# Two transformer blocks on one core: the first attention moves issued ahead of the biases, batch 1's first norm moved behind the first maxima and onto GpSimd, one cross load two rounds later

## The chip, the cores and the metric

The kernel runs on one core of one Trainium2 chip. A core has five engines, each with its own instruction queue: TensorE (PE, matrix products; PEld is its weight load), VectorE (DVE), ScalarE (ACT), GpSimd (POOL) and SyncE (SP, which here only issues DMAs). ACT and POOL can issue DMAs as well. Instructions of one queue run in the order written; between queues, semaphores order them. The metric is the device time of one execution in microseconds (us), lower is better.

## The reference

Two layers, each with self attention, cross attention and a gated feed-forward, every one behind a layer norm and with a residual. 4 batches of 512 tokens, 320 wide; 20 heads of 16; a context of 1601 rows of 192 for the cross attention; all float32.

```python
h1 = _ln(x, n1_g, n1_b)
x = _attn(h1, h1, q1, k1, v1, o1_w, o1_b, heads) + x
h2 = _ln(x, n2_g, n2_b)
x = _attn(h2, context, q2, k2, v2, o2_w, o2_b, heads) + x
h3 = _ln(x, n3_g, n3_b)
proj = h3 @ ff_w1 + ff_b1
a, g = jnp.split(proj, 2, axis=-1)
ff = a * jax.nn.gelu(g, approximate=False) @ ff_w2 + ff_b2
return ff + x
```

## The kernel before, in words

A program in Python writes the instruction order of every engine out by hand. An attention is cut into **units**: one batch and one group of four heads (five groups per batch, so 20 units of self and 20 of cross attention per layer). A unit goes through these steps:

- `add_proj`: queries and keys from the normed tokens (`qkps`, L908). The result is split into a high and a low half in the tile `halves` (L919 and L920 for the very first unit, L924 with POOL's L827 and L828 for the others) and moved by DMA into the layout of the products, `kT` and `q` (L876, "the moves").
- `add_values`: the values (`vps`, L1035, copied into `vals` at L1017), two parts of 4 pieces each for a batch: 128 wide, then 192 wide.
- `max_pairs` / `round_of`: a first pass of score products (`sps`, L1076) that serves only for the maxima of the rows, taken by DVE (L1087). A round of self attention is 8 products and 4 maxima; a unit has 4 rounds.
- `max_end`: the negated maxima are split, turned (L1163) and moved by four small DMAs into `nrows` (L1171).
- `main`: the scores again (`st`, L1324) with the maxima added by a third product that reads `nrows`, the exponential on ACT (L1334), then probabilities times values (`av`, L1350), summed by ACT (L1364, L1369) and POOL (L1370). The pass of maxima of the next unit is woven in between.
- `add_finish`: once the five units of a batch are done, the sums are inverted, and three loads (`aT` L1224 with `rT` L1225, issued by SP) bring the output back; POOL divides (L1232), PE projects (`ops`, L1250). There are only two buffers for `rT`, so the third load waits until POOL has divided the first; what stands behind it in SP's queue waits with it.

`add_norm` makes the layer norm. For the first self attention: statistics (DVE, L561 and L562), an inverse root by a guess and three refinements (`guess_root`, `better_root`, L521 to L537), `plain` (L625, twelve pieces that subtract and scale), and `turn` (L639, twelve transposes by PE into `hps`, brought to `hT` by ACT and DVE at L647 and L645). `biased` (L618) adds the output bias to the residual on POOL. The flag `start["on"]` holds during the beginning and puts root and `plain` on DVE; afterwards they are POOL's.

After the beginning, work is taken from chains by due times counted in **rounds** (two rounds to a step of `main`); a task may also ask that so many rounds have passed since another, as `since(i, n)` does in `add_finish`. The beginning itself, at the end of the function, is a list of calls in order: load batch 0 and the weights, two bias rows (`brow`) and batch 1; norm, project and move unit 0; then unit 1, the norm of batch 1, unit 2, the four rounds of unit 0's maxima with products in between, two rounds of unit 1, and from there the main loop.

Of the kernel before, what the change touches and what calls it, by code (L numbers as in the profile page):

```python
# [23 lines left out]
P = 128  # L24
NQ = N // P
# [53 lines left out]
def kernel(ctx: ExitStack, tc: tile.TileContext, x, context, ws, out):  # L79
# [18 lines left out]
    nc = tc.nc  # L98
# [109 lines left out]
    def now(fs):  # L208
        for f in fs:
            f()  # L210
# [153 lines left out]
    units = []  # L364
# [48 lines left out]
    def bank(name):  # L413
        i = min(range(NB), key=lambda i: bank_free[i])
        assert bank_free[i] < HELD, name
        t = psum.tile([P, 512], F32, tag=f"bank{i}", name=name)
        bank_of[id(t)] = [i, t, bank_free[i], 0.0]
        bank_free[i] = HELD
        return t

    def written(us, *tiles):
        expect["pe"] = max([expect["pe"]] + [bank_of[id(t)][2] + 0.05 for t in tiles]) + us
        for t in tiles:
            bank_of[id(t)][3] = expect["pe"] + 0.17
# [17 lines left out]
    def add(chain, cost, f, due, ready=yes, soon=yes):  # L442
        chains[chain].append((cost if isinstance(cost, tuple) else (cost,), due, ready, soon, f))
# [71 lines left out]
            assert chains[name], name  # L515
            run(name)

    def guess_root(var):

        a, h, y, z = (two.tile([P, NQ], F32, tag=f"root{i}", name=f"root{i}") for i in range(4))  # L520
        nc.vector.tensor_scalar(a, var, EPS, None, ALU.add)  # L521
        nc.vector.tensor_scalar(
            z.bitcast(I32), a.bitcast(I32), 1, None, ALU.logical_shift_right
        )
        nc.vector.tensor_scalar(y.bitcast(I32), z.bitcast(I32), -1, 0x5F3759DF, ALU.mult, ALU.add)
        eng = nc.vector if start["on"] else nc.gpsimd
        eng.tensor_scalar(h, a, -0.5, None, ALU.mult)
        return h, y, z

    def better_root(h, y, z):  # L530


        eng = nc.vector if start["on"] else nc.gpsimd
        eng.tensor_tensor(z, y, y, ALU.mult)
        eng.tensor_tensor(z, z, h, ALU.mult)
        eng.tensor_scalar(z, z, 1.5, None, ALU.add)
        eng.tensor_tensor(y, y, z, ALU.mult)  # L537

    hn_used = []
    EARLIER = 14  # L540


# [8 lines left out]
    def add_norm(l, b, i, put, done, due):  # L551
# [12 lines left out]

        def root(step):
            if step == 0:
                s["root"] = guess_root(s["mv"][:, :, 1])
                s["rstd"] = s["root"][1]
            for _ in range(step + 1):
                better_root(*s["root"])  # L570
            s["round"] = clock["round"]

        def normalise(t):
# [43 lines left out]
        def biased(t):  # L617
            nc.gpsimd.tensor_tensor(xb[:, t, :], xb[:, t, :], brow[(3 * l + i) % 2], ALU.add)  # L618

        def plain(t):  # L620
            if t == 0:
                s["hn"] = one.tile([P, DB, NQ, SLOT], F32, tag="hturned", name="hturned").rearrange("p k t w -> p (k t w)")
            for k, at, n in HK:
                w = n // SLOT
                (nc.vector if start["on"] else nc.gpsimd).tensor_scalar(  # L625
                    s["hn"][:, t * D + at : t * D + at + n].rearrange("p (d k) -> p k d", k=w),
                    xb[:, t, at : at + n].rearrange("p (k d) -> p k d", k=w),
                    s["mv"][:, t, 0:1], s["rstd"][:, t : t + 1], ALU.subtract, ALU.mult,
                )
            if start["on"]:  # L630
                busy("dve", 0.45)
            s["round"] = clock["round"]

        def turn(k, at, n):
            if k == 0:
                place()
            ps = bank("hps")
            for t in range(NQ):
                nc.tensor.transpose(ps[:n, t * P : (t + 1) * P], s["hn"][:, t * D + at : t * D + at + n], ident)  # L639
            written(0.5, ps)  # L640
            busy("act", 0.7, ps)
            to = s["hT"][:n, k].rearrange("p (i t w) -> p t i w", t=NQ, w=SLOT)
            src = ps[:n].rearrange("p (t i w) -> p t i w", t=NQ, w=SLOT)
            if start["on"] and k == 1:
                nc.vector.tensor_scalar(to, src, lng[i][:n, k : k + 1], lnb[i][:n, k : k + 1], ALU.mult, ALU.add)  # L645
            else:
                nc.scalar.activation(to, src, AF.Identity, bias=lnb[i][:n, k : k + 1], scale=lng[i][:n, k : k + 1])  # L647
            if k == 2:
                for t in range(NQ):
                    biased(t)  # L650
                hn_used.remove(b)
                put(s["hT"])

# [498 lines left out]
    def max_end(u):  # L1152

        top, high, low = (u.nm[:, :, i, :] for i in range(3))
        nc.vector.tensor_reduce(
            high.bitcast(F32R), top.rearrange("p j (t o) -> p j t o", o=1), AX.X, ALU.max, negate=True
        )
        nc.vector.tensor_reduce(
            low, u.nm[:, :, 0:2, :].rearrange("p j e t -> p j t e"), AX.X, ALU.add, negate=True
        )  # L1160
        turned = two.tile([P, SLOT], F32, tag="turned", name="turned")

        nc.vector.transpose(turned.rearrange("p (j c) -> p j c", j=HG), u.nm[:, :, 1:3, :].rearrange("p j e t -> p j (e t)"))  # L1163
        busy("dve", 0.6)
        slots = u.rows.bitcast(F32).rearrange("(g s) n -> s g n", s=DH)[0].rearrange("g (t r) -> g t r", t=NQ)

        def rows():
            for i in range(P // SLOT):
                part = slice(i * SLOT, (i + 1) * SLOT)
                queue = (nc.sync, nc.scalar, nc.gpsimd, nc.sync)[i] if start["on"] else nc.sync  # L1170
                queue.dma_start(out=slots[:, :, part], in_=turned[part, :])  # L1171

        if u.cross and u.before.cross:
            u.rows_of = rows
            errands.appendleft((clock["round"] + 1, yes, rows))
        else:
            rows()

    def add_finish(u):
# [3 lines left out]
        def since(i, n):  # L1183
            return lambda: len(when) > i and clock["round"] >= when[i] + n
# [29 lines left out]
        def read():  # L1214

            held["read"] += 1
            held["open"] += 1
            aT = one.tile([P, 3, N], F32, tag="aT", name="aT")
            way, part = o_way[u.b % 2], {}

            def load(k, at, n):
                heads = slice(at // DH, (at + n) // DH)
                part[k] = two.tile([P, N], F32, tag="rT", name="rT")
                dma(out=aT[:n, k, :], in_=way[:DH, heads])  # L1224
                dma(  # L1225
                    out=part[k][:n],
                    in_=r_way[u.b % 2][heads].rearrange("(o j) n -> o j n", o=1).to_broadcast([DH, n // DH, N]),
                )
                when.append(clock["round"])

            def divide(k, n):
                nc.gpsimd.tensor_tensor(aT[:n, k, :], aT[:n, k, :], part[k][:n], ALU.mult)  # L1232

            for k, at, n in DK[:2]:
                load(k, at, n)
            first, second, third = DK
            add("divide", 0.0, lambda: divide(0, first[2]), r - 20, yes, since(4, 3))
            add("divide", 0.0, lambda: divide(1, second[2]), r - 20)
            add("divide", 0.0, lambda: load(*third), r - 20, yes, since(4, 5 if u.l else 7))
            add("divide", 0.0, lambda: divide(2, third[2]), r - 20, yes, since(5, 3))  # L1240
            add("divide", 0.0, lambda: end(aT), r - 20)

# [440 lines left out]
    take_rooms(0)  # L1683
    now(load_x(0))
    now(load_self(0))
    load_bias(0, 0)
    load_bias(0, 1)
    now(load_x(1))

    add_norms(0)  # L1690
    add_proj(units[0])
    warm(5)
    until(lambda: not chains["proj"], "proj")
    at_once(units[0])
    add_proj(units[1])
    add_values(units[0])
    run("proj")
    run("proj")
    for _ in range(2 * NQ + 2):
        run("norm")  # L1700
    at_once(units[1])
    add_proj(units[2])
    first = units[0]
    first.pairs = max_pairs(first)
    for chain in ("proj", "proj", "values", None):
        round_of(first.pairs[0].popleft()[1] + first.pairs[1].popleft()[1])
        if chain:
            run(chain)

    at_once(units[2])  # L1710
    run("values")
    max_reduce(first)
    max_end(first)
    loads.extend(load_x(2))
    for fs in (load_out(0, "o1_w"), load_x(3), load_cross(0)):
        loads.extend(fs)
    second = units[1]
    second.pairs = max_pairs(second)
    for _ in range(2):
        round_of(second.pairs[0].popleft()[1] + second.pairs[1].popleft()[1])  # L1720
        run("values")
        run("values")
    start["on"] = False
    clock["credit"] = 0.0

# [47 lines left out]
```

## Time and profile before

| what | value |
|---|---|
| median of 3 runs | 2929.41 us (2924.77 to 2933.03) |
| the profiled execution | 2929.68 us, of which the span from first to last instruction is 2927.9 us |
| PE busy | 2863.1 us, 98% of the span |
| first 100 us of the span | PE busy 86.94 us, granted clock 0.88 |

Times in the profile count from the start of the span. In rows of the timeline stand: start, length, engine, line, operation, output<-inputs, shapes, count, and in brackets the idle time of that engine before and what ended it. Rows with a count join neighbours of one kind. In rows of the windows stand: the stretch, its length, busy time and instructions of PE, PEld, DVE, ACT and POOL, the clock granted to PE (1.00 is full), the share of the 16 DMA engines that was busy, and GB/s. The engine called SPq or ACTq is that engine's queue, whose rows are DMA issues.

### The profile page before, as it was taken

The page shows a single profiled execution, that of the slowest core. Times are in us where ns is not written, and L with a number is a line of the kernel's source. Part 1 is how long each engine was busy: PE and PEld are TensorE (multiplying, and loading weights), DVE is VectorE, ACT ScalarE, POOL GpSimd, SP SyncE. Part 2 cuts the span into 40 slices and gives each one's busy share as a digit, 9 for nine tenths or more (in the row PEclk, how much of TensorE's full clock was granted, in tenths as well). Part 3 has the DMA queues.
Part 4 walks back from the last instruction along what each step waited for, and adds up shares of the span by engine and source line. Part 5 has one row for each costly group of instructions (what it writes and reads, how often), then busy time and mean ns, then how long its engine had stood idle before and what let it go on. Part 6 is the DMA issues. An engine that isn't in the chain of part 4 may idle for free.

```text
span 2927.9 us, 83288 instructions
## 1 busy us (share of the span) xinstructions
PE 2863.1 (98%) x35018; PEld 1545.3 (53%) x35018; DVE 1980.7 (68%) x3752; ACT 1950.1 (67%) x4033; POOL 1299.5 (44%) x1409
## 2 busy tenths in 40 slices
PE   8999999999999999999999999999999999999999
PEld 4445555555555555355554555555555555544554
DVE  7776878788788878323257678788778888762221
ACT  3777678887888888500138776788888888893000
POOL 3556345555555645211125653455455564451110
PEclk8999999999999999999999999999999999999999
DMA  3443224232232222200113432221122122122000
GB/s 106 111 123 98 67 71 105 59 82 63 51 92 62 54 54 62 84 18 11 36 44 88 109 98 66 68 65 49 54 65 50 47 72 63 42 59 72 20 23 14
DMA packets 163494, 188.59 MB, mean 64 GB/s; under 512 B 61988, under 2 KB 109104, under 8 KB 163120
## 3 DMA queue, kind: packets, MB, share of 16 engines
q1 hardware_dynamic: 162616, 181.69, 24.3%
q8 instruction: 275, 4.51, 0.6%
q10 hardware_dynamic: 472, 1.58, 0.2%
q14 instruction: 99, 0.81, 0.1%
q0 software_dynamic: 32, 0.00, 0.0%
HBM read 55.76 MB, written 29.36 MB: 29 GB/s over the span
## 4 chain that ended last, share of the span: by engine, by line
PE 85%; DVE 6%; POOL 4%; issue 2%; DMA 2%; ACT 1%; SPq 1%; POOLq 0%; ACTq 0%; DVEq 0%
PE av L1350 21%; PE st L1324 19%; PE fps L1435 10%; PE sps L1076 8%; PE yps L1542 6%; PE vps L1035 5%; PE ops L1250 3%; PE kps L972 3%; PE qkps L908 3%; PE fps L1495 3%; DVE nmax L1087 2%; DVE pm L1087 2%; PE qps L947 2%; POOL o L1370 1%; PE sps L1101 1%
## 5 line engine op out<-in xcount | busy, mean ns | idle before, releaser
L1334 ACT ACTIVATE pr<-st 128x512 f32<-128x512 f32 (+1 forms) x2720 | 1404.5, 604 | 327.1 <-PE st L1324 297.0
L1087 DVE TENSOR_REDUCE pm<-sps 128x1 f32<-128x512 f32 (+1 forms) x1920 | 1149.0, 660 | 251.0 <-PE sps L1076 243.8
L1370 POOL TENSOR_TENSOR o<-o,vo 128x512 f32<-128x512 f32 x576 | 739.8, 1284 | 936.9 <-ACT vo L1369 922.1
L1076 PE MATMUL sps<-kT,q 32*128 32x450 f32 (+1 forms) x4800 | 870.7, 422 | 10.7 <-DMA q<-halves 4.3
L1324 PE MATMUL st<-q,kT 32*128 32x512 f32 (+1 forms) x5120 | 791.1, 420 | 2.0 <-ACT o L1364 1.6
L1350 PE MATMUL av<-pr,vals 128*32 128x512 f32 (+1 forms) x5440 | 734.8, 606 | 30.7 <-DVE pm L1087 7.2
L1324 PEld LDWEIGHTS st<-q,kT 32*128 32x128 f32 (+1 forms) x5120 | 448.6, 180 | 293.9 <-ACT pr L1334 115.4
L1324 PE MATMUL st<-nrows,ones 32*128 32x512 f32 (+1 forms) x2720 | 560.8, 398 | 7.1 <-DMA nrows<-turned 7.0
L1087 DVE TENSOR_REDUCE nmax<-sps 128x1 f32<-128x512 f32 x640 | 397.2, 682 | 120.6 <-PE sps L1076 115.2
L1076 PEld LDWEIGHTS sps<-kT,q 32*128 32x128 f32 x4800 | 434.6, 184 | 69.5 <-ACT pr L1334 12.8
L1369 ACT COPY vo<-av 128x512 f32<-128x512 f32 x576 | 352.9, 613 | 15.2 <-PE av L1350 8.5
L1506 ACT ACTIVATE gl<-fps,b 128x512 f32<-128x512 f32 x80 | 54.7, 687 | 409.0 <-PE fps L1495 301.1
L1435 PE MATMUL fps<-hT,w 128*128 128x512 f32 x640 | 283.5, 597 | 0.0
L1324 PEld LDWEIGHTS st<-nrows,ones 32*128 32x128 f32 (+1 forms) x2720 | 263.3, 180 | 18.7 <-issue 6.2
L1350 PEld LDWEIGHTS av<-pr,vals 128*32 128x32 f32 (+1 forms) x5440 | 110.9, 108 | 304.3 <-DVE pm L1087 186.7
L1507 DVE SCALAR_TENSOR_TENSOR hid<-fps,b,gl 128x512 f32<-128x512 f32 x80 | 59.7, 748 | 247.5 <-ACT gl L1506 245.4
L1435 PEld LDWEIGHTS fps<-hT,w 128*128 128x128 f32 x640 | 119.1, 190 | 155.0 <-issue 152.3
L1542 PE MATMUL yps<-w,hid 128*128 128x320 f32 x640 | 175.7, 434 | 0.0
L1542 PEld LDWEIGHTS yps<-w,hid 128*128 128x128 f32 x640 | 120.5, 190 | 56.3 <-ACT gl L1506 5.3
L1250 PEld LDWEIGHTS ops<-wo,aT 112*32 112x32 f32 (+1 forms) x3072 | 97.9, 110 | 61.9 <-issue 30.0
L1250 PE MATMUL ops<-wo,aT 112*32 112x160 f32 (+1 forms) x3072 | 124.9, 300 | 4.1 <-POOL aT L1232 3.8
L1111 DVE TENSOR_REDUCE pm<-sps 128x4 f32<-128x508 f32 x160 | 98.9, 681 | 36.1 <-PE sps L1101 33.0
(89 smaller groups left out, 2459.5 us busy)
## 6 DMA issues: line engine op xcount, KB each, us to landing
kT<-stages SPq DMA_DIRECT2D x80, 400.5 KB
oway<-o SPq DMA_DIRECT2D x80, 256.0 KB
q<-halves SPq DMA_DIRECT2D x80, 256.0 KB
q<-halves SPq DMA_DIRECT2D x27, 512.0 KB
kT<-halves SPq DMA_DIRECT2D x40, 256.0 KB
aT<-oway SPq DMA_DIRECT2D x32, 224.0 KB
rT<-rway SPq DMA_DIRECT2D x32, 224.0 KB
hT<-hturned SPq DMA_DIRECT2D x96, 64.0 KB
```

Source lines behind the costliest of these rows:

```text
L1035: nc.tensor.matmul(ps[f : f + m, :w], lhsT=u.kvT[:n, k, at + f : at + f + m], rhs=wv[:n, k, h0 * DH : h1 * DH], start=(k == 0), stop=(k == ...
L1076: nc.tensor.matmul(own[0][:, :w], lhsT=u.queries(slice(j * SLOT, (j + 1) * SLOT), e, t), rhs=u.kT[j * SLOT : (j + 1) * SLOT, u.k0 + at : u ...
L1087: nc.vector.tensor_reduce(to, own[0][:, :w], AX.X, ALU.max)
L1111: nc.vector.tensor_reduce(u.pm[:, :, j, ns - 1], ps[:, : NQ * w].rearrange("p (t w) -> p t w", w=w)[:, :, :n], AX.X, ALU.max,)
L1250: nc.tensor.matmul(ps[f : f + m, : D // 2], lhsT=aT[:n, k, f * NQ + t * SLOT : f * NQ + t * SLOT + m], rhs=wo[:n, k, cols], start=(k == 0) ...
L1324: nc.tensor.matmul(own[0][:r, :], lhsT=ones[rows, :r] if e == 2 else u.keys(rows, c), rhs=u.rows[rows, :] if e == 2 else u.queries(rows, e ...
L1334: nc.scalar.activation(p[:r], own[0][:r], AF.Exp)
L1350: nc.tensor.matmul(ps[j * SLOT : (j + 1) * SLOT, :], lhsT=columns_of[:r, head : head + SLOT], rhs=pr.pop((c, j))[:r, :], start=True, stop= ...
L1369: nc.scalar.copy(vo, ps)
L1370: nc.gpsimd.tensor_tensor(u.o, u.o, vo, ALU.add)
L1435: nc.tensor.matmul(ps, lhsT=w1[:, k, i * FF + c * P : i * FF + (c + 1) * P], rhs=natural(u.hT[:, k]), start=start, stop=stop,)
L1542: nc.tensor.matmul(ps[:, :D], lhsT=hid[c][:, t * P : (t + 1) * P], rhs=w2[:, c, :], start=(c == 0), stop=(c == NHC - 1),)
```

## The change

- In the beginning, the two `brow` loads and batch 1's four tiles of tokens are issued behind unit 0's moves instead of before them.
- More products by PE whose result nobody reads (`wps`): 7 in place of 5 at the start, and one between the transposes of batch 0's first chunk (three in all).
- All four first pieces of values stand directly behind the projections of units 0 and 1, ahead of the first round of maxima; the two 192-wide pieces that were in the beginning are left to the main loop.
- Batch 1's norm is cut out of its place ahead of the maxima. Its statistics stand on DVE behind unit 0's `max_end`; its root and its twelve pieces of `plain` are on POOL.
- Batch 0's additions of the bias row are held back behind unit 1's moves.
- One round of unit 1's maxima, rather than two, stands ahead of the main loop.
- The first `nrows` are moved by SP and ACT, two each, in place of SP, ACT, POOL, SP.
- In `add_finish`, the third load of layer 1's cross attention is issued 7 rounds behind the first two in place of 5 (layer 0 had 7 already).

```diff
@@ guess_root(var, b), better_root(h, y, z, b)
-        eng = nc.vector if start["on"] else nc.gpsimd
+        eng = nc.vector if start["on"] and not b else nc.gpsimd
...
@@ plain(t)
-                (nc.vector if start["on"] else nc.gpsimd).tensor_scalar(
+                (nc.vector if start["on"] and not b else nc.gpsimd).tensor_scalar(
...
@@ turn(k, at, n)
             ps = bank("hps")
+            idle = bank("wps") if start["on"] and k == 0 else None
             for t in range(NQ):
                 nc.tensor.transpose(ps[:n, t * P : (t + 1) * P], s["hn"][:, t * D + at : t * D + at + n], ident)
+                if idle is not None and t + 1 < NQ:
+                    nc.tensor.matmul(idle[:, :P], lhsT=ident, rhs=fill[:, :P], start=True, stop=True)
+            if idle is not None:
+                busy("act", 0.0, idle)
...
                 for t in range(NQ):
-                    biased(t)
+                    if start["on"] and not b:
+                        held_back.append(lambda t=t: biased(t))
+                    else:
+                        biased(t)
...
@@ max_end(u)
-                queue = (nc.sync, nc.scalar, nc.gpsimd, nc.sync)[i] if start["on"] else nc.sync
+                queue = nc.scalar if start["on"] and i % 2 else nc.sync
...
@@ add_finish(u)
-            add("divide", 0.0, lambda: load(*third), r - 20, yes, since(4, 5 if u.l else 7))
+            add("divide", 0.0, lambda: load(*third), r - 20, yes, since(4, 5 if u.l and not u.cross else 7))
...
@@ the beginning
     now(load_x(0))
     now(load_self(0))
-    load_bias(0, 0)
-    load_bias(0, 1)
-    now(load_x(1))
 
     add_norms(0)
     add_proj(units[0])
-    warm(5)
+    warm(7)
     until(lambda: not chains["proj"], "proj")
     at_once(units[0])
     add_proj(units[1])
     add_values(units[0])
+    load_bias(0, 0)
+    load_bias(0, 1)
+    now(load_x(1))
     run("proj")
     run("proj")
-    for _ in range(2 * NQ + 2):
-        run("norm")
+    for _ in range(4):
+        run("values")
     at_once(units[1])
+    for f in held_back:
+        f()
     add_proj(units[2])
     first = units[0]
     first.pairs = max_pairs(first)
-    for chain in ("proj", "proj", "values", None):
+    for chain in ("proj", "proj", None, None):
         round_of(first.pairs[0].popleft()[1] + first.pairs[1].popleft()[1])
         if chain:
             run(chain)
 
-    at_once(units[2])
-    run("values")
     max_reduce(first)
     max_end(first)
+    at_once(units[2])
+    for _ in range(6):
+        run("norm")
...
-    for _ in range(2):
+    for _ in range(1):
         round_of(second.pairs[0].popleft()[1] + second.pairs[1].popleft()[1])
-        run("values")
-        run("values")
+    for _ in range(10-6):
+        run("norm")
```

The change also moves every later line number by up to 12. Three places show what it does to the queues. First, DVE around unit 0's maxima (`nmax_95`), before; `x_108` is batch 1:

```order
L625 TENSOR_SCALAR hturned<-x_108,mv,root_318 128x4x32
L625 TENSOR_SCALAR hturned<-x_108,mv,root_318 128x3x32 x2
L1087 TENSOR_REDUCE nmax_95<-sps 128x1 x16
L1155 TENSOR_REDUCE nmax_95<-nmax_95 128x4x4
L1158 TENSOR_REDUCE nmax_95<-nmax_95 128x4x4
L1163 STREAM_TRANSPOSE turned<-nmax_95 128x32
```

Here batch 1's norm (its last two rows are shown) stands ahead of the sixteen maxima. The same place on DVE now:

```order
L929 SCALAR_TENSOR_TENSOR halves<-qkps,scales,halves 128x256 x2
L1096 TENSOR_REDUCE nmax_95<-sps 128x1 x16
L1164 TENSOR_REDUCE nmax_95<-nmax_95 128x4x4
L1167 TENSOR_REDUCE nmax_95<-nmax_95 128x4x4
L1172 STREAM_TRANSPOSE turned<-nmax_95 128x32
L562 BN_STATS st_473<-x_108 128x6
L563 BN_AGGR mv<-st_473 128x2
```

The maxima follow the first unit's split directly, and batch 1's statistics come behind them. Its root, the first of three refinements, now on POOL behind unit 2's split:

```order
L837 TENSOR_TENSOR halves<-halves 128x512
L527 TENSOR_SCALAR root_486<-root_485 128x4
L534 TENSOR_TENSOR root_488<-root_487 128x4
L535 TENSOR_TENSOR root_488<-root_488,root_486 128x4
L536 TENSOR_SCALAR root_488<-root_488 128x4
L537 TENSOR_TENSOR root_487<-root_487,root_488 128x4
```

Two more refinements, the twelve pieces L626 and the four additions L619 follow on POOL; none of these but the additions was POOL's before.

Second, PE behind batch 0's transposes (`q_102` and `q_103` are the queries of units 0 and 1), now:

```order
L641 MATMUL hps<-ident,hturned 96x128 x8
L917 MATMUL qkps<-hT,wqk 32x256 x48
L1044 MATMUL vps<-wv_112,hT 32x128 x48
L1085 MATMUL sps<-kT_101,q_102 128x512 x8
L917 MATMUL qkps<-hT,wqk 32x256 x12
```

The four pieces of values (L1044), which were spread between the rounds of maxima, fill the place ahead of the first round. Further on, PE's rows around batch 1's transposes, now:

```order
L1333 MATMUL st<-nrows_97,ones 128x512 x2
L1085 MATMUL sps<-kT_101,q_103 128x512 x2
L641 MATMUL hps<-ident,hturned 128x128 x4
L641 MATMUL hps<-ident,hturned 96x128 x8
L1333 MATMUL st<-q_102,kT_101 128x512 x2
```

The transposes `hps` of batch 1 stand where they stood before: behind the first scores of unit 0 and ahead of all the rest of the main loop.

Third, SP at the end of a batch in layer 1's cross attention, before:

```order
L1225 DMA rT<-rway_132 112x1x512
L1224 DMA aT<-oway_130 96x1x512
L1225 DMA rT<-rway_132 96x1x512
L1171 DMA nrows_97<-turned 8x4x32 x4
L1191 DMA oway_131<-o 4x32x512
```

The next unit's `nrows` stand behind the third load (96 partitions). The same place now:

```order
L1234 DMA rT<-rway_132 112x1x512
L1180 DMA nrows_97<-turned 8x4x32 x4
L1233 DMA aT<-oway_130 96x1x512
L1234 DMA rT<-rway_132 96x1x512
L1200 DMA oway_131<-o 4x32x512
```

The third load has gone behind them; the two first loads have not moved.

More of the change, by code (lines that the diff above doesn't have):

```diff
@@ L516, in until, with guess_root @@
             run(name)
-    def guess_root(var):
+    def guess_root(var, b):
         a, h, y, z = (two.tile([P, NQ], F32, tag=f"root{i}", name=f"root{i}") for i in range(4))
@@ L525, in guess_root, with better_root @@
         nc.vector.tensor_scalar(y.bitcast(I32), z.bitcast(I32), -1, 0x5F3759DF, ALU.mult, ALU.add)
-        eng = nc.vector if start["on"] else nc.gpsimd
+        eng = nc.vector if start["on"] and not b else nc.gpsimd
         eng.tensor_scalar(h, a, -0.5, None, ALU.mult)
         return h, y, z
-    def better_root(h, y, z):
-        eng = nc.vector if start["on"] else nc.gpsimd
+    def better_root(h, y, z, b):
+        eng = nc.vector if start["on"] and not b else nc.gpsimd
         eng.tensor_tensor(z, y, y, ALU.mult)
@@ L539 @@
     hn_used = []
+    held_back = []
     EARLIER = 14
@@ L566, in root @@
             if step == 0:
-                s["root"] = guess_root(s["mv"][:, :, 1])
+                s["root"] = guess_root(s["mv"][:, :, 1], b)
                 s["rstd"] = s["root"][1]
             for _ in range(step + 1):
-                better_root(*s["root"])
+                better_root(*s["root"], b)
             s["round"] = clock["round"]
```

## The prediction

> **What bounds the kernel now.** I read the page first, then the chain of waits in order of time for the beginning, then SP's queue and PE's waits at the ends of the batches in layer 1.
>
> ```profile
> span 2927.9 us, 83288 instructions
> PE 2863.1 (98%) x35018; PEld 1545.3 (53%) x35018; DVE 1980.7 (68%) x3752; ACT 1950.1 (67%) x4033; POOL 1299.5 (44%) x1409
> ```
>
> PE is busy nearly everywhere, so a change that removes no product can win only PE's idle time, 65 us in all, and what PE loses at a low clock. The chain through the beginning shows whose idle time this change touches:
>
> ```profile
> 13.41 5.25 DMA x<-in_x_dram
> ...
> 25.61 3.39 DVE hturned L625 x12
> ...
> 43.51 4.00 PE vps L1035 x48
> ...
> 50.49 1.46 PE hps L639 x12
> ```
>
> It goes over batch 1: its tokens, its norm on DVE, unit 0's maxima behind that norm, values at a low clock, then batch 1's transposes. From there it is PE, piece after piece. So I compare both kernels at one point, where PE leaves the transposes and takes unit 0's second chunk of scores: 51.9 us now.
>
> ```profile
> 50.42 1.53 PE L639 MATMUL hps<-ident,hturned 128*128 128x128 f32 x12
> 51.88 0.49 PE L1324 MATMUL st<-q,kT 32*128 32x512 f32 x2
> ```
>
> **Part 1, layer 1's cross load.** The ends of its batches, and last the same place in layer 0, which has the seven rounds already:
>
> ```profile
> 2076.60 0.21 DVE L1163 STREAM_TRANSPOSE turned<-nmax 128x32 f32<-128x32 f32 x1
> 2078.99 0.54 SPq L1225 DMA_DIRECT2D rT<-rway  x1
> 2079.64 2.65 SPq L1171 DMA_DIRECT2D nrows<-turned  x4
> 2083.49 0.49 PE L1324 MATMUL st<-nrows,ones 32*128 32x512 f32 x2 [0.86 <-DMA nrows<-turned]
> 2293.14 0.49 PE L1324 MATMUL st<-nrows,ones 32*128 32x512 f32 x2 [1.08 <-DMA nrows<-turned]
> 2502.64 0.50 PE L1324 MATMUL st<-nrows,ones 32*128 32x512 f32 x2 [0.87 <-DMA nrows<-turned]
> ...
> 845.50 2.65 SPq L1171 DMA_DIRECT2D nrows<-turned  x4
> 848.20 0.70 SPq L1224 DMA_DIRECT2D aT<-oway  x1
> ```
>
> The turned maxima were ready at 2076.81, but SP stood on the third `rT`, which waits for POOL's first division, until 2079.53. The four `nrows` left 2.8 us late, and PE waited 0.86 us for them, 1.08 and 0.87 at the next two batches. With the load behind the `nrows`, as in layer 0, these 2.8 us go: **-2.8** (bounds -3.5, if it frees something behind, and 0, if another wait takes their place). The division and the projection come two rounds later; nothing reads them before the feed-forward. The fourth batch ends inside the feed-forward, where no `nrows` follow: 0.
>
> **Part 2, the first moves and what they were behind.** Unit 0's moves and the DMA engines around them:
>
> ```profile
> 18.35 18.31 SPq L876 DMA_DIRECT2D kT<-halves  x3
> 24.18 1.23 PE L1076 MATMUL sps<-kT,q 32*128 32x512 f32 x8 [4.32 <-DMA q<-halves]
> ...
> 18.50:19.00 0.50, 0.50 (x16) 0.25 (x10) 0.31 (x1) 0.00 (x0) 0.50 (x2) 1.00 0.89 312
> 19.00:19.50 0.50, 0.50 (x16) 0.24 (x8) 0.47 (x3) 0.44 (x1) 0.50 (x1) 1.00 0.24 87
> 23.00:23.50 0.50, 0.00 (x0) 0.00 (x0) 0.47 (x4) 0.00 (x0) 0.16 (x1) 0.50 0.08 25
> ```
>
> The biases and tokens were through by 19.2: the engines fall to 0.24 there, then carry the moves alone until 23.0. The moves waited for `halves`, not for them. So the new order takes nothing away from the 5.8 us between issue and first product; it puts two `brow` and four `x` into SP's queue behind `kT`, beside `q` in ACT's, and sharing the engines with them can cost `q` up to about a third of its 3.5 us (19.5 to 23.0). Against it, the extra `wps` may hold PE's clock:
>
> ```profile
> 11.50:12.00 0.50, 0.01 (x2) 0.01 (x1) 0.50 (x3) 0.00 (x0) 0.00 (x0) 0.50 0.81 202
> 11.99 2.18 PE L639 MATMUL hps<-ident,hturned 128*128 128x128 f32 x9 [0.49 <-DVE hturned L625]
> ```
>
> Nine transposes at clock 0.50 took 2.18 us; at full clock half, so the projections and the issue come up to 0.9 us sooner. I set these against each other: first product at 24.2 as before (bounds 23.3 and 25.4).
>
> **Part 3, unit 0's maxima without the norm ahead of them.**
>
> ```profile
> 25.34 2.79 PE L908 MATMUL qkps<-hT,wqk 128*32 128x256 f32 x24
> 28.88 4.86 DVE L1087 TENSOR_REDUCE nmax<-sps 128x1 f32<-128x512 f32 x8
> 34.74 4.88 DVE L1087 TENSOR_REDUCE nmax<-sps 128x1 f32<-128x512 f32 x8 [0.99 <-PE sps L1076]
> 55.07 0.74 PE L1076 MATMUL sps<-kT,q 32*128 32x512 f32 x8
> 42.12 1.38 PE L1076 MATMUL sps<-kT,q 32*128 32x512 f32 x7 [1.39 <-ACT vals L1017]
> 42.00:42.50 0.50, 0.38 (x4) 0.38 (x7) 0.50 (x2) 0.24 (x2) 0.50 (x2) 0.67 0.12 13
> 48.50:49.00 0.50, 0.50 (x11) 0.29 (x3) 0.29 (x1) 0.00 (x0) 0.00 (x0) 0.51 0.00 0
> ```
>
> Sixteen maxima are 9.7 us, and they can now start with the first round. How tightly they follow depends on PE's clock. Values fill PE up to about 22, then it waits some 2 us for the moves. In this trace a wait of 1.39 us (ending at 42.12) was enough: the clock is 0.67 in the half microsecond after 42.00 and 0.50 until 49.0. So I take the clock as lost at the next step. A round is then 1.23 us in place of 0.74 and a projection 2.79 us, and DVE waits for them twice: first round 24.2 to 24.9, projection to 27.7, second round to 28.95, projection to 31.75, third and fourth round behind; the maxima end at 37.5 instead of 39.6. With the clock kept they would run through, 24.2 + 0.8 + 9.7 = 34.8. The Trainium skill speaks for the second ("TensorE: Matmul & The Clock Gate", section "What's actually happening"): the clock is gated to half only after an idle window of about 3.4 us, and by that rule the sum would be that of the first rival below. The trace disagrees, with 1.39 us; the windows there are mixed, not idle.
>
> **Part 4, batch 1's norm behind the maxima, on POOL.** What its steps take, from DVE's own and from batch 2's norm, which is on POOL already:
>
> ```profile
> 40.08 0.21 DVE L1163 STREAM_TRANSPOSE turned<-nmax 128x32 f32<-128x32 f32 x1
> 18.69 0.49 DVE L561 BATCH_NORM_STATS2 st<-x 128x6 f32<-128x320 f32 x1 [0.36 <-DMA x<-in_x_dram]
> 21.22 0.62 DVE L521 TENSOR_SCALAR root<-mv 128x4 f32<-128x4 f32 x1
> 97.53 0.17 DVE L521 TENSOR_SCALAR root<-mv 128x4 f32<-128x4 f32 x1
> 97.80 0.25 POOL L527 TENSOR_SCALAR root<-root 128x4 f32<-128x4 f32 x1 [0.63 <-DVE root L521]
> 98.19 0.20 POOL L534 TENSOR_TENSOR root<-root 128x4 f32<-128x4 f32 x1
> 99.07 0.20 POOL L537 TENSOR_TENSOR root<-root,root 128x4 f32<-128x4 f32 x1
> 105.83 4.38 POOL L625 TENSOR_SCALAR hturned<-x,mv,root 128x128 f32<-128x128 f32 x6
> ```
>
> Ending the maxima 0.7 us (39.6 to 40.3), statistics 2.5 (18.7 to 21.2), three steps of the root on DVE 0.3 and the way to POOL, together 0.7, then on POOL 0.4 and three refinements of 1.15 (a step every 0.29) = 3.9, and twelve pieces at 4.38 / 6 = 0.73 are 8.75, against 3.39 on DVE. Another 0.3 for the last transposes, which follow each piece. Sum 16.8: PE leaves the transposes at 37.5 + 16.8 = 54.3 instead of 51.9, **+2.4** (bounds -0.3 with the clock kept, +4). This is the wait that takes the place of the old one: the transposes stand in PE's queue ahead of unit 0's second chunk, and scores, `av`, exponentials and every later product queue behind them. The first scores come sooner, but nothing is won by it. The new way of the `nrows` (SP and ACT, two each) ends long before the transposes and costs nothing; the held-back additions on POOL lie ahead of the root, in its idle time.
>
> **Part 5, work that moved behind that point.**
>
> ```profile
> 66.00 2.14 PE L1035 MATMUL vps<-wv,hT 128*32 128x192 f32 x48
> ```
>
> Two pieces of 192-wide values (2.0 us at full clock) and one round of maxima (0.7) now come after 51.9, where PE is the chain: **+2.7** (bounds 2.0, if they fill waits, and 4.8 at half clock). The four 128-wide pieces went into PE's wait for the moves and are in part 3 already.
>
> **Part 6, the clock after the wait.** PE now waits some 8 us before the transposes, and starts into the main loop at half clock. Before, it needed from 42.1 to 49.0, all but 1.4 us of it work, to get the clock back. Two steps of 3.4 us (the distance between the changes at 42.2 and 49.0 halved), the first partly past, are 4.2 us at half speed: **+2.1** (bounds 0.8 and 4.2).
>
> **Sum:** -2.8 + 0 + 2.4 + 2.7 + 2.1 = +4.4 us on the profiled execution's own 2929.7 us (1.8 more than its span), which is 0.3 above the median of 2929.4: **2934**.
>
> **The rivals.**
>
> *The clock holds through the wait for the moves.* Maxima end at 34.8, the transposes at 51.6 (-0.3), and with the other terms +1.7: 2931. For it: the extra products and values leave PE less idle than before. Against it: the clock lost behind 1.39 us.
>
> *The first scores decide, not the transposes.* If POOL's norm were through in time, the loop would start when the `nrows` land: 37.5 + 0.7, 2.65 to issue four (2079.64) and 1.2 to land (2083.49) are 42.0, in place of 47.5 when the values end in the chain. -5.5 + 2.7 - 2.8 make 2924. For it: DVE is rid of the norm's 6 us ahead of the maxima. Against it: 0.73 us for each of twelve pieces on POOL.
>
> *Slower: DVE holds up POOL's pieces.* At 21.22 a root step on DVE took 0.62 instead of 0.17 us while POOL worked, and POOL's 25 new instructions run beside DVE's maxima. If each waited for half a maximum (0.3 us), +7.7: 2942. From 0.18 us an instruction it is slower by more than the bound below. Against it is a row:
>
> ```profile
> 34.85 1.26 POOL L828 TENSOR_TENSOR halves<-halves 128x512 f32<-128x512 f32 x1
> ```
>
> It ran beside the eight maxima of 34.74, which took 4.88 us, as the eight with POOL idle took 4.86. The Trainium skill ("SBUF — State Buffer", section "SBUF: two separate sides") has the two engines lock a port pair against each other for a whole instruction, but only where DVE needs its second port. The trace agrees for both cases: the root waited, the maxima, which read PSUM, did not.
>
> *The cross load wins nothing* (the `nrows` then wait for something else): 2937.
>
> **How the numbers follow.** Forecast 0.55, clock held 0.22, first scores 0.08, POOL held up 0.10, cross load nothing 0.05. A measurement of this kernel tells 0.3%, or 8.8 us, from no change. Forecast and clock held stay inside, up to some spread of the median, as the three runs of before spread by 8 us; only the third rival is clearly beyond. So: faster 0.04, same 0.81, slower 0.15. The range 2927 to 2939 holds the forecast and the first rival with their bounds, and leaves out the second and third.
>
> **What would show it.** In the profile after: batch 1's transposes end at 54 (right) or before 51 (wrong), with POOL's pieces as what ended PE's wait; maxima from 25 to 37.5; clock 0.5 behind the first product and again behind the transposes; no wait for `nrows` at the batch ends of layer 1. The prediction is wrong if PE does not wait at the transposes, or if any place other than these differs by more than 2 us.

## The result and the profile after

| | median of the runs | runs | ratio to before (95% interval) |
|---|---|---|---|
| before | 2929.36 us (2921.93 to 2933.03) | 22 | |
| after | 2923.80 us (2919.10 to 2929.62) | 22 | 0.9982 (0.9976 to 0.9987) |

The change wins 5.3 us (3.8 to 7.0), 0.18%: less than the 0.3% within which I called a result no change, but a gain, where the forecast was a loss of 4.4 us, and below the range of 2927 to 2939. The profiled execution after has a span 3.7 us shorter:

```profile
span 2924.2 us, 83307 instructions
PE 2865.2 (98%) x35028; PEld 1548.0 (53%) x35028; DVE 1969.1 (67%) x3727; ACT 1951.1 (67%) x4033; POOL 1309.9 (45%) x1433
```

In the rows of the changed kernel below, the same lines have numbers up to 9 higher than before. The beginning after the change, from the timelines of PE, DVE and POOL:

```profile
23.50 0.74 PE L1085 MATMUL sps<-kT,q 32*128 32x512 f32 x8 [2.08 <-issue]
27.39 7.50 DVE L1096 TENSOR_REDUCE nmax<-sps 128x1 f32<-128x512 f32 x12 [0.66 <-PE sps L1085]
38.65 0.79 PE L1333 MATMUL st<-nrows,ones 32*128 32x512 f32 x2 [2.73 <-DMA nrows<-turned]
42.11 8.65 POOL L626 TENSOR_SCALAR hturned<-x,mv,root 128x128 f32<-128x128 f32 x12
49.52 2.18 PE L641 MATMUL hps<-ident,hturned 128*128 128x128 f32 x9 [1.67 <-POOL hturned L626]
51.63 0.79 PE L1333 MATMUL st<-q,kT 32*128 32x512 f32 x2
```

The first product comes at 23.5, unit 0's maxima end at 34.9 (27.39 + 7.50), POOL's twelve pieces take 8.65 us, and PE leaves batch 1's transposes at 51.6, against 51.9 before. So the maxima are 4.7 us earlier and PE is not: POOL's norm has taken the place of what was saved. PE also runs at half clock from 35.2 to 55.7, as the windows show (clock in the third column from the end):

```profile
35.50:36.00 0.50, 0.42 (x4) 0.00 (x0) 0.47 (x3) 0.00 (x0) 0.00 (x0) 0.50 0.00 0
...
55.00:55.50 0.50, 0.50 (x8) 0.00 (x0) 0.50 (x1) 0.37 (x1) 0.00 (x0) 0.50 0.00 0
56.00:56.50 0.50, 0.50 (x8) 0.16 (x8) 0.00 (x0) 0.50 (x1) 0.00 (x0) 1.00 0.00 0
```

A marker that both kernels have is the moment at which DVE turns the maxima of a unit (80 times, L1163 before). I use the second unit's, and two in layer 1's cross attention: the one where the first finished batch is fetched back (2076.60 before, quoted in the prediction) and the last unit's. What lies between these two is called **the stretch** from here on. Before and after:

```profile
58.65 0.21 DVE L1163 STREAM_TRANSPOSE turned<-nmax 128x32 f32<-128x32 f32 x1
...
2619.10 0.21 DVE L1163 STREAM_TRANSPOSE turned<-nmax 128x32 f32<-128x32 f32 x1
```

```profile
62.83 0.21 DVE L1172 STREAM_TRANSPOSE turned<-nmax 128x32 f32<-128x32 f32 x1
...
2080.81 0.21 DVE L1172 STREAM_TRANSPOSE turned<-nmax 128x32 f32<-128x32 f32 x1
...
2616.21 0.21 DVE L1172 STREAM_TRANSPOSE turned<-nmax 128x32 f32<-128x32 f32 x1
```

The new kernel is 4.2 us late at the second unit (62.83 - 58.65), still 4.2 late where the stretch begins (2080.81 against 2076.60), and 2.9 early where it ends. The stretch is 535.40 us long in place of 542.50: 7.1 us shorter, not 2.8. PE's waits in it (the view counts from 2070 to 2622; line, what it waited for, us in total, times, longest), before and then after:

```profile
PE av L1350 <- DVE pm L1087: 3.4, 5, 1.2
PE st L1324 <- DMA nrows<-turned: 2.8, 3, 1.1
```

```profile
PE av L1359 <- ACT pr L1343: 0.6, 3, 0.2
PE av L1359 <- DVE pm L1096: 0.4, 2, 0.2
```

The `nrows` waits of 2.8 us are gone, as forecast. Gone too are 3 us of waits behind DVE's maxima (`pm`), of which the prediction said nothing.

### The profile page after: what moved, and what is told of

Its sections match the earlier page's. It is cut to its first block, busy times and chain, and to the rows that moved or that the text cites. A ratio compares the mean times of both kernels' runs of the same rounds, so it can differ in the third digit from the quotient of the medians.

```text
span 2924.2 us, 83307 instructions
## 1 busy us (share of the span) xinstructions
PE 2865.2 (98%) x35028; PEld 1548.0 (53%) x35028; DVE 1969.1 (67%) x3727; ACT 1951.1 (67%) x4033; POOL 1309.9 (45%) x1433
## 4 chain that ended last, share of the span: by engine, by line
PE 87%; DVE 5%; POOL 4%; issue 1%; DMA 1%; ACT 1%; SPq 0%; POOLq 0%; ACTq 0%; DVEq 0%
PE av L1359 22%; PE st L1333 20%; PE fps L1444 10%; PE sps L1085 9%; PE yps L1551 6%; PE vps L1044 5%; PE kps L981 4%; PE ops L1259 3%; PE qkps L917 3%; PE fps L1504 3%; DVE nmax L1096 2%; PE qps L956 2%; POOL o L1379 1%; PE sps L1110 1%; DVE pm L1096 1%
```

## What those other waits are

The timelines of DVE, POOL and PE before the change, some 50 us behind the end of the first batch:

```profile
2131.16 0.52 DVE L521 TENSOR_SCALAR root<-mv 128x4 f32<-128x4 f32 x1
2131.72 1.26 DVE L522 TENSOR_SCALAR root<-root 128x4 int32<-128x4 int32 x1
2133.01 0.17 DVE L525 TENSOR_SCALAR root<-root 128x4 int32<-128x4 int32 x1
2133.09 2.41 DVE L1087 TENSOR_REDUCE pm<-sps 128x1 f32<-128x450 f32 x4
```

```profile
2129.76 1.89 POOL L828 TENSOR_TENSOR stages<-stages 128x801 f32<-128x801 f32 x1
2131.66 1.29 POOL L1370 TENSOR_TENSOR o<-o,vo 128x512 f32<-128x512 f32 x1
```

```profile
2133.76 1.07 PE L1350 MATMUL av<-pr,vals 128*32 128x512 f32 x8 [1.17 <-DVE pm L1087]
```

The three small steps of a norm's root take 0.17 us each elsewhere. Here the first ends at 2131.68, where POOL's operation L828 ends (2131.65), and the second at 2132.98, where POOL's addition L1370 ends (2132.95). DVE stood still for POOL, the maxima queued behind the root came late, and PE waited 1.17 us for them. Steps of 1.26 and 1.27 us stand at 2341 and 2557 too, ahead of PE's waits of 1.17 and 0.60 us at 2343 and 2559. The Trainium skill ("SBUF — State Buffer", section "SBUF: two separate sides") describes this as an exclusive lock on a port pair which an operation of DVE in a two-port mode and one of GpSimd hold for the whole instruction; the ends, 0.03 us apart, agree. The prediction cited the same rule and showed a root step that took 0.62 us beside POOL, but it priced only the other direction, DVE holding up POOL.

With the cross load alone moved (the first experiment below), the same steps stand ahead of the addition and of POOL's splitting of the keys (L827), and are short:

```profile
2127.50 0.16 DVE L521 TENSOR_SCALAR root<-mv 128x4 f32<-128x4 f32 x1
2127.69 0.17 DVE L522 TENSOR_SCALAR root<-root 128x4 int32<-128x4 int32 x1
2127.89 0.17 DVE L525 TENSOR_SCALAR root<-root 128x4 int32<-128x4 int32 x1
```

```profile
2127.99 1.29 POOL L1370 TENSOR_TENSOR o<-o,vo 128x512 f32<-128x512 f32 x1 [1.83 <-ACT vo L1369]
2129.23 0.85 POOL L827 CAST stages<-stages 128x801 fp32r<-128x801 f32 x1
```

The edit does not touch the norm. But the projections go two rounds back in the order, and statistics, roots and conversions, which are placed by rounds around them, fall elsewhere; root and addition no longer meet.

## The experiments

All ratios are to the kernel before, run on the same chip in the same job.

### The two halves of the change

Edit of the first, on the kernel before:

```diff
-            add("divide", 0.0, lambda: load(*third), r - 20, yes, since(4, 5 if u.l else 7))
+            add("divide", 0.0, lambda: load(*third), r - 20, yes, since(4, 5 if u.l and not u.cross else 7))
```

> The kernel before with one edit, layer 1's cross load seven rounds behind. Theory A (two waits went with it: SP's nrows, 2.8 us, and the small root steps of DVE that stand in a lock behind GpSimd's additions, 1.17 + 1.17 + 0.60 us at 2134, 2343 and 2559 us, which miss each other once the two rounds shift): 6 to 7 us less than before, no wait of PE above 0.3 us at those places. Theory B (the prediction's part 1: the nrows alone): 2.8 us less, and the three waits behind DVE's pm stay.

Measured: 2921.36 us, ratio 0.9975 (0.9964 to 0.9985), 7.3 us less (4.4 to 10.5). Run again later:

> The kernel before with layer 1's cross load seven rounds behind, a second time, beside the next kernel on the same chip. Theory A: 6 to 7.5 us less than before, as the first time.

2921.62 us, 0.9976 (0.9967 to 0.9985), 7.0 us less. The stretch, by the marker:

```profile
2074.86 0.21 DVE L1163 STREAM_TRANSPOSE turned<-nmax 128x32 f32<-128x32 f32 x1
...
2610.43 0.21 DVE L1163 STREAM_TRANSPOSE turned<-nmax 128x32 f32<-128x32 f32 x1
```

535.57 us, as after the change (535.40), and 535.56 in the second execution; no wait of PE in it exceeds 0.3 us. Theory A holds, B falls.

The other half is the changed kernel with that one line put back:

```diff
-            add("divide", 0.0, lambda: load(*third), r - 20, yes, since(4, 5 if u.l and not u.cross else 7))
+            add("divide", 0.0, lambda: load(*third), r - 20, yes, since(4, 5 if u.l else 7))
```

> The changed kernel with layer 1's cross load put back to five rounds: the new beginning alone. Theory A (the beginning costs what the prediction's parts 3 to 6 say with the clock held, -0.3 + 2.7 + 2.1): 4 to 4.5 us more than before, the turned maxima of the second unit 4.2 us later. Theory C (the beginning is itself the gain, the shift seen in the trace being lost again or another execution's): 2 to 3 us less than before.

Measured: 2931.49 us, ratio 1.0005 (0.9996 to 1.0014): 1.5 us more (1.2 less to 4.1 more). The stretch is back at 542.4 us, and the second unit is late, 2.5 us behind that of the trace before:

```profile
61.14 0.21 DVE L1172 STREAM_TRANSPOSE turned<-nmax 128x32 f32<-128x32 f32 x1
...
2078.97 0.21 DVE L1172 STREAM_TRANSPOSE turned<-nmax 128x32 f32<-128x32 f32 x1
...
2621.39 0.21 DVE L1172 STREAM_TRANSPOSE turned<-nmax 128x32 f32<-128x32 f32 x1
```

C falls by its size: the beginning brings no gain of 2 to 3 us. A's 4 to 4.5 us is at the end of the interval, and its second unit 4.2 us late is 2.5 here. The two halves add up, -7.3 + 1.5 = -5.8 against -5.3 measured together. Within these intervals the whole gain is that of the cross load.

### SP's queue by itself

The kernel before, with the third load of layer 1 at its old round, issued by POOL:

```diff
+                issue = nc.gpsimd.dma_start if u.l and u.cross and at == DK[2][1] else dma
-                dma(out=aT[:n, k, :], in_=way[:DH, heads])
-                dma(
+                issue(out=aT[:n, k, :], in_=way[:DH, heads])
+                issue(
```

> The kernel before, with the third cross load of layer 1 at its old round but issued by GpSimd, behind its own division, so that SP never stands on it and no projection or norm moves. Theory A: the three nrows waits of 0.86, 1.08 and 0.87 us go (2.8 us), the waits behind the root steps (1.17, 1.17, 0.60) stay, since root and addition keep their rounds: 3 us less than before. Theory H (all 7 us hang on SP alone): 6 to 7 us less. Theory I (the wait moves to GpSimd's issue of the load, whose additions the av chain follows): no less than before.

Measured: 2925.84 us, ratio 0.9988 (0.9980 to 0.9997), 3.5 us less (0.9 to 5.9). The `nrows` leave SP at once, and POOL issues the load behind its division:

```profile
2076.74 2.64 SPq L1171 DMA_DIRECT2D nrows<-turned  x4
```

```profile
2077.53 2.56 POOL L1233 TENSOR_TENSOR aT<-aT,rT 112x512 f32<-112x512 f32 x2
...
2081.24 0.59 POOL L1225 DMA_DIRECT2D aT<-oway  x1
```

PE's waits in the stretch, and the marker:

```profile
PE av L1351 <- DVE pm L1087: 3.4, 5, 1.2
```

```profile
2076.46 0.21 DVE L1163 STREAM_TRANSPOSE turned<-nmax 128x32 f32<-128x32 f32 x1
...
2615.25 0.21 DVE L1163 STREAM_TRANSPOSE turned<-nmax 128x32 f32<-128x32 f32 x1
```

The `nrows` waits are gone and the 3.4 us behind `pm` stand unchanged. The stretch is 538.79 us, 3.7 shorter. So of the 6.9 us that the cross load alone takes off the stretch, 3.7 hang on SP's queue, and the other 3.2 on the shift of the order; the waits behind the root (1.17 + 1.17 + 0.60 = 2.9) would be nearly all of that, which the next experiment tests. H and I fall. The `nrows` were worth 3.7 and not the 2.8 of their waits: by the marker the three batch ends give 1.13, 1.42 and 1.15 us for recorded waits of 0.86, 1.08 and 0.87. Why each gives more than its wait is open.

### The lock by itself

The kernel before, with the first root steps of the main loop on POOL. The edit also makes one step of the shift and the subtraction, in the beginning too, where these steps stay on DVE:

```diff
-        nc.vector.tensor_scalar(a, var, EPS, None, ALU.add)
-        nc.vector.tensor_scalar(
-            z.bitcast(I32), a.bitcast(I32), 1, None, ALU.logical_shift_right
-        )
-        nc.vector.tensor_scalar(y.bitcast(I32), z.bitcast(I32), -1, 0x5F3759DF, ALU.mult, ALU.add)
         eng = nc.vector if start["on"] else nc.gpsimd
+        eng.tensor_scalar(a, var, EPS, None, ALU.add)
+        eng.tensor_scalar(y.bitcast(I32), a.bitcast(I32), -0.5, 0x5F3759DF, ALU.mult, ALU.add)
```

> The kernel before with the first steps of every root in the main loop on GpSimd (the added constant, and one step in place of the shift and the subtraction), so that no two-port operation of DVE can stand behind GpSimd's additions. Theory A (a root step of DVE that meets an addition waits until its end, and PE's av waits behind the maxima that queue after it: 2.0, 1.3, 0.75, 0.55, 1.17, 1.17 and 0.60 us in the trace of before): 6 to 8 us less than before, DVE's waits gone. Theory D (the long root steps lie in DVE's slack): within 1 us of before.

Measured: 2925.22 us, ratio 0.9984 (0.9975 to 0.9992), 4.7 us less (2.3 to 7.3). D falls; A's 6 to 8 is at the upper end. In layer 1's cross attention the waits behind `pm` shrink to 0.4 us in two places, and the `nrows` waits grow from 2.8 to 3.4:

```profile
PE st L1321 <- DMA nrows<-turned: 3.4, 3, 1.6
...
PE av L1347 <- DVE pm L1084: 0.4, 2, 0.2
```

The stretch is 540.06 us, 2.4 shorter. By the marker, the three units in which root steps had met POOL are 1.18, 1.15 and 0.56 us shorter, 2.9 together, so the waits behind the root are worth what was read from them. The second batch end gives 0.5 us back: its four `nrows` took 2.90 us to issue in place of 2.65, with POOL's division as far behind the marker as before (1.07 us); why is open. This execution lies 4.7 us below the median of its runs, and its trace has two more gains that are not those of the edit alone: 3.6 us ahead of the second unit, where the clock stays full that was at half from 42.2 to 49.0 before, and 3.1 us between it and the stretch, where the clock is at half for 6.8 us in place of 13.7.

### The norm on DVE

The changed kernel with batch 1's norm at its new place, but on DVE; the same edit stands in `guess_root`, `better_root` and `plain`:

```diff
-        eng = nc.vector if start["on"] and not b else nc.gpsimd
+        eng = nc.vector if start["on"] else nc.gpsimd
```

> The changed kernel with batch 1's norm still behind the first maxima, but on DVE. Theory A (GpSimd's chain of 16.8 us decides the beginning: twelve pieces of 0.72 and the refinements of 3.9; on DVE the pieces take 3.4 and the root some 2): PE leaves batch 1's transposes at about 44 in place of 51.6, and the whole is 7 to 8 us less than the changed kernel, 12 to 13 less than before. Theory E (the nrows, the values or another wait of PE decides): within 2 us of the changed kernel, 4 to 7 less than before.

Measured: 2922.79 us, ratio 0.9976 (0.9967 to 0.9985): 7.0 us less than before. That is 1.7 less than the changed kernel by the two ratios, whose intervals overlap. A's 12 to 13 falls; E's total holds, at its edge, but not its reason alone. PE and DVE:

```profile
38.98 0.79 PE L1333 MATMUL st<-nrows,ones 32*128 32x512 f32 x2 [3.03 <-DMA nrows<-turned]
41.64 1.82 PE L1333 MATMUL st<-q,kT 32*128 32x512 f32 x4 [1.87 <-DVE nmax L1096]
46.19 2.18 PE L641 MATMUL hps<-ident,hturned 128*128 128x128 f32 x9 [0.34 <-DVE hturned L626]
48.30 0.79 PE L1333 MATMUL st<-q,kT 32*128 32x512 f32 x2
```

```profile
40.90 2.48 DVE L1096 TENSOR_REDUCE nmax<-sps 128x1 f32<-128x512 f32 x4
43.29 3.38 DVE L626 TENSOR_SCALAR hturned<-x,mv,root 128x128 f32<-128x128 f32 x12
```

POOL's chain did decide: PE leaves the transposes at 48.3 in place of 51.6. But 3.3 us came of it and not 7.6, because unit 1's round of maxima (2.48 us) now stands in DVE's own queue between root and pieces, and PE waits at half clock for the `nrows` and then for that round.

### The products of no use, and the order of the loads

Two edits on the changed kernel. The first:

```diff
-            idle = bank("wps") if start["on"] and k == 0 else None
+            idle = None
...
-    warm(7)
+    warm(5)
```

The second, ahead of `add_norms(0)` and behind `add_values(units[0])`:

```diff
+    load_bias(0, 0)
+    load_bias(0, 1)
+    now(load_x(1))
...
-    load_bias(0, 0)
-    load_bias(0, 1)
-    now(load_x(1))
```

> The changed kernel without its products of no use (five warming products in place of seven, none between batch 0's transposes). Theory A (they hold the clock before the first product, which came 0.7 us sooner with them, and are free otherwise): first product back to 24.2, PE leaves batch 1's transposes 0.7 us later, total within 1 us of the changed kernel. Theory J (they are what keeps the clock up through the first rounds): maxima end at 37.5 as in the prediction's part 3, 2.5 us more than the changed kernel.

> The changed kernel with the biases and batch 1's tokens issued ahead of unit 0's moves again, as before the change; everything else changed. Theory A (the prediction's part 2: the moves wait for halves, not for these loads; the first product comes 0.7 us earlier by the clock, not by the order): first product at 23.5 still, total within 1 us of the changed kernel. Theory K (the loads ahead of the moves cost their issue time on SP): first product at 24.2 or later, 0.7 us or more on top.

Without the products: 2925.24 us, ratio 0.9981 (0.9972 to 0.9990). With the loads first: 2925.02 us, 0.9980 (0.9971 to 0.9988). Both are the changed kernel's 0.9982. The first product, of the one and of the other:

```profile
24.74 0.80 PE L1085 MATMUL sps<-kT,q 32*128 32x512 f32 x8 [2.08 <-issue]
```

```profile
23.23 0.74 PE L1085 MATMUL sps<-kT,q 32*128 32x512 f32 x8 [1.80 <-DMA q<-halves]
```

In these executions the useless products bring it 1.2 us forward, and the new order of the loads brings nothing. J and K fall: without the products the maxima end at 36.4 and not 37.5, and with the loads first the first product is not late. What the products bring at the front cannot be told from nothing in the total.

### The cross load and the root steps together

The kernel before with two of the edits above together, that of the cross load and that of the root steps; of its beginning only the root is touched, by one step fewer on DVE:

> The kernel before with layer 1's cross load seven rounds behind and the first root steps of the main loop on GpSimd, the beginning untouched. Theory A (in layer 1's cross attention both edits remove the same 2.4 us of lock waits, else they add up): -7.3 - 4.7 + 2.4, about 9.5 us less than before, and no wait of PE above 0.5 us in that stage. Theory F (they remove different things): 12 us less. Theory G (the gain of the root steps was the clock of the beginning alone, which one execution keeps and another loses): 7 us less, as the cross load alone.

> The cross load and the root steps together, a second time. Theory A (the root steps meet GpSimd's additions in layer 0's cross attention too, where waits of 2.0, 1.3 and 0.75 us are seen before): 2 to 3 us less than the cross load alone, so 9 to 10 less than before. Theory G (nothing is left once the cross load has moved): the same as the cross load alone.

Measured: 2920.09 us, ratio 0.9966 (0.9954 to 0.9979), and the second time 2918.67 us, 0.9963 (0.9951 to 0.9976), where the cross load alone had 0.9976: 10.8 us less than before (7.0 to 14.3), and by the ratios some 5 less than the changed kernel. A's 9.5 us fits, and F's 12 and G's 7 lie inside the intervals too, so the share of the root steps is not measured well. The traces show where they win and where they cost. In layer 0's cross attention (the view counts from 595 to 1150) PE's waits behind `pm`, before and then in both executions:

```profile
PE av L1350 <- DVE pm L1087: 3.3, 2, 2.0
```

```profile
PE av L1347 <- DVE pm L1084: 1.5, 2, 1.2
```

The wait of 2.0 us is gone, and so is one of 0.75 us behind another operation of DVE; of that of 1.3 us, 1.2 stay. With the cross load alone the 3.3 us stand. In layer 1's cross attention the root steps cost, so that theory A's "no wait above 0.5 us" there fails; PE's waits, and what stands on DVE and POOL:

```profile
PE av L1347 <- DVE pm L1084: 1.8, 2, 0.9
```

```profile
2132.51 0.51 DVE L582 STREAM_TRANSPOSE hturned<-hn 128x320 f32<-128x320 f32 x1 [1.23 <-POOL hn L574]
```

The stretch is 536.9 us in both executions, 1.3 longer than with the cross load alone: POOL has more to do ahead of the norm, DVE waits 1.23 us for it in order, and the maxima behind that are late again.

## Why the prediction was wrong

**Part 1 (-2.8) failed first.** It measured -7.1 in the trace and -7.0 and -7.3 in the runs. The step that failed is the sentence that the division and projection come two rounds later and nothing reads them before the feed-forward. That is true of the data and was not the question: the tasks that moved with them no longer met the work on the engines that they had met before. The terms are 3.7 for the `nrows` (SP's queue alone), put at 2.8 because a wait of PE was counted at its recorded length, and 3.2 for a second set of waits. The list of PE's waits in this stretch showed that set ahead of the change, and larger than the `nrows`, 3.4 against 2.8 us; the part went by the ends of the batches alone. This step is not the whole miss: with -7.1 in its place the sum is +0.1, still no gain. The rest is the beginning, which parts 2 to 6 put at +7.2 us and the timed runs of the beginning alone at +1.5 (1.2 less to 4.1 more). Part 3 took 2.7 of that too much; some 3 us stay open.

**Part 2 (0) was right** on the loads. The first product came at 23.5, inside the bounds; the gain came from the useless products, as the part said it might.

**Part 3 took the wrong end.** The step that failed is that the clock, once lost at the next step, stays at half through all four rounds. The clock did fall, but only from 25.0 to 28.4, and DVE waited for PE once, for 0.66 us. The maxima ended at 34.9, not at 37.5. That it is the 34.8 of the rival in which the clock holds is in part luck: the first product, 0.7 us earlier than that rival took it, made up for the wait.

**Part 4 was right in its working:** from the maxima's end to PE's leaving 16.74 us against 16.8 added up from rows, 8.65 against 8.75 for the pieces. PE left at 51.6 because part 3 came out early; the rival had 51.6.

**Parts 5 and 6 (+2.7 and +2.1) fit the trace together:** -0.3 + 2.7 + 2.1 = 4.5, and the second unit is 4.2 us late. Behind the transposes PE ran at half clock for 4.1 us (51.6 to 55.7), as part 6 had it with 4.2. They do not fit the timed runs well: the beginning alone costs 1.5 us there. What gives the rest back is open. Four traces of the unchanged beginning put the second unit's turn anywhere from 55.9 to 58.7 us, two of the new one put it at 61.1 and 62.8, and the profiled execution after lies 2.2 us above the median of its runs, so one pair of executions cannot settle 3 us. Of the moves in the beginning only the norm's engine, the useless products and the order of the loads had a run of their own.

**The rivals.** "The clock holds" was right on the transposes (51.6), though the clock did not hold, and with 7.1 in place of 2.8 it comes to 2927, 3 us above the median. "The first scores decide" gave 2924, the measured time, for a reason that did not occur: the transposes decided. POOL's pieces were not held up (0.72 us each), and the cross load won something. No rival held a larger gain elsewhere. I had asked whether another wait would take the place of the one removed; that another might go with it had only the bound of -3.5 in part 1.

**The chances** put 0.81 on a result within 0.3%, which it is. The range was too narrow below: part 1's lower bound of -3.5 left no room for what a shifted order can free.

## What to carry to other kernels

When an edit moves tasks in a hand-made order, list every wait of the stage before, not just the one aimed at: the others stand or fall with who meets whom, and either sign is possible. An operation of 0.17 us on a queue in order is worth the length of what it may stand behind, here 1.26 us of another engine's addition. And work moved out of an engine's way gives little if the same tasks then stand on a slower engine in that path, as batch 1's norm did.

## What the runs showed of the hardware

Two things that the prediction did not price. The first is the lock above in this direction: a DVE step on 4 elements for each partition, 0.17 us elsewhere, waits out a 128x512 addition of POOL, to within 0.03 us of its end, and with it everything queued on DVE.

The second is the clock. In part 3 I took from a wait of 1.39 us that such a wait costs the clock. The same place (PE waits for the copies of the values, then makes 48 products for 192-wide values), before the change and then with the third load on POOL, where the beginning is untouched:

```profile
43.44 4.07 PE L1035 MATMUL vps<-wv,hT 128*32 128x192 f32 x48
```

```profile
42.46 0.89 PE L1076 MATMUL sps<-kT,q 32*128 32x512 f32 x7 [1.71 <-ACT vals L1017]
43.28 2.17 PE L1035 MATMUL vps<-wv,hT 128*32 128x192 f32 x48
```

A longer wait, 1.71 us, left the products at full speed, 2.17 us, and 1.39 had them at half, 4.07 us. With one root step fewer in the beginning, it was 1.72 and 2.17. So the length of the wait alone does not decide. The Trainium skill ("TensorE: Matmul & The Clock Gate", section "What's actually happening") says that the activity window runs free of the program; differences between executions of one beginning agree with that, though no run here set the phase on purpose. One reading fits this place, and no run tests it: the clock changed at 35.3, 42.2 and 49.0 in the trace before, and after the change at 25.0 and 28.4, half as far apart. Counted in steps of 3.4 us, the wait of 1.39 lies inside one step (38.8 to 42.2). With the load on POOL the clock rose at 35.0, and the wait of 1.71 (40.75 to 42.46) is parted by the end of a step at 41.8. Waits of 1.16 and 1.14 us, in two of the executions with root steps on POOL, lie inside one step and did not cost the clock, so they would have to be too short. Whatever the rule, the clock lost behind the 1.39 us, from which part 3 reasoned, is a thing that one execution has and another has not. The half clock of the new beginning is not: it lasts 20.5 us both after the change (35.2 to 55.7) and with the beginning alone (32.7 to 53.2).
